# Layer 0's mixture of experts: the second half of two experts' outputs goes back to its nodes by one-hot products instead of a store and gathers

## The chip, the cores and the metric

The kernel runs on one core of a Trainium2 chip. The time is the device time of one execution in microseconds, and the median of several executions is compared. The core has TensorE (PE: matrix products and transposes, into PSUM), VectorE (DVE), ScalarE (ACT), GpSimd (POOL) and SyncE (SP). SP, ACT and POOL issue the transfers (DMA).

## The reference, cut to what matters

Two layers work on 384 nodes with 1024 features each, in float32. Each layer adds a graph block and an attention block to x, and then a mixture of experts. The change lies at the end of layer 0: in its mixture of experts (8 experts, hidden width 352, two experts per node) and in the norm that opens layer 1.

```python
x = x + _L0_ffn_ref(_layernorm(x, axis=-1)[None], ...)[0]     # _L0_ffn_ref:
    top_logits, idx = jax.lax.top_k(logits, TOP_K)            # TOP_K = 2
    scores = jax.nn.softmax(top_logits, axis=-1)
    for e in range(E):                                        # E = 8
        a, g = jnp.split(x_rep @ w1[e].T, 2, axis=-1)
        he = jax.nn.silu(a) * g @ w2[e].T
        out = out + jnp.where((expert_ids == e)[:, None], he, 0)
    out = out * scores.reshape(-1, 1)
    combined = out.reshape(N, TOP_K, h).sum(axis=1)
xn = _layernorm(x, axis=-1)
x = x + _L1_gnn_ref(xn, ...) + _L1_mix_ref(xn[None], ...)[0]
```

So every node's row of x receives two expert rows, each with a weight of its own, before layer 1 can normalize it.

## The kernel before

The nodes lie in three blocks of 128 (NB = 3), one node per partition. x stays in SBUF for the whole run, as does `keep`, a set of small tiles that pass from stage to stage. [...]

**Routing.** `to_places` chooses the two experts of each node and gives it a place in each: expert e has 128 places (CAP0), and place r of expert e is row e * 128 + r of a table in HBM. `keep["slots"]` holds the two row numbers of each node and `keep["share"]` the two weights. The normalized rows are scattered to their places in `xg0`.

**Experts** (`experts0_sorted`). For each expert, `rows_of` loads its 128 rows (POOL's queue) and transposes them on PE (L906). `hidden_of` multiplies them with w1 (L915), and ACT and DVE form the gated hidden rows (L918, L919). `by_feature` transposes these (L925) into `hT` (L926 on DVE, L927 on ACT). The loop runs hidden(e), rows(e + 1), by_feature(e), so that PE has work while the other engines finish. PSUM has three buffers with the tag "t" for all transposes and five with the tag "h" for products. After the loop, for each half and each expert, three products give the expert's 128 x 512 output `y` (L942; the last of the three has depth 96). ACT copies `y` to `ys` (L945) and its own queue stores it in `yg0[hf]` (L946). After the first half, `take(0, nb)` gathers, for each block, the two expert rows of each node from `yg0[0]` (POOL, L306), and DVE adds them to x with their weights (L959).

**The opening of layer 1** (`layer1`). `take(1, nb)` does the same for the second half, just ahead of the norm of the same block: DVE's statistics (L169, L171), ACT's square root (L177), and the norm itself, half on DVE (L201) and half on ACT (L202). `to_t` transposes the normed block on PE (L215, copied by L216), and two halves of products with `w_gnn` follow (L1011). The blocks go one after another; `issue_after` keeps the additions of the next block behind the norm of this one. After the last gather, POOL loads `a_bc` and `ed_w`, and the loads of `w_k` and `w_v` on SP's queue are held until that gather has landed (`held`).

**The order.** Each engine runs its own queue in order. The queues are filled at compile time by a planner, which takes the instructions in the order of the text but lets one go ahead when it expects those before it still to be waiting. Weight tiles come from a ring of buffers, and SP loads the next one as soon as its buffer is free.

Of the kernel before, what the change touches and what calls it, by code (L numbers as in the profile page):

```python
# [10 lines left out]
F32 = mybir.dt.float32  # L11
I32 = mybir.dt.int32
AF = mybir.ActivationFunctionType
OP = mybir.AluOpType
# [3 lines left out]
P = 128  # L18
N = 384
NB = N // P  # L20
D = 1024
KC = D // P
HB = 512
# [5 lines left out]
X = 8  # L29
# [4 lines left out]
CAP0 = 128  # L34
CAP = 64
MORE = 2
LAST = 1
K2 = (128, 128, 96)
PIECE = 1024
# [5 lines left out]
def gps_two_layers(ctx: ExitStack, tc: tile.TileContext, d, out: bass.AP):  # L45
    nc = tc.nc
# [366 lines left out]
    with ExitStack() as layer:  # L413
# [317 lines left out]
        def row(cols, name, dtype=F32):  # L731
            return kp.tile([P, *cols], dtype, name=name)

        keep = {"xe0": [row([KC // 2, P], f"xe0_{g}") for g in range(2)], "oh": row([NB, X], "oh4"), "own": row([NB, P], "own4"), "most": row([NB], "most4"),
                "slot": row([NB], "slot4", I32), "own_e": row([NB], "own_e4", I32), "info": row([NB, 2], "info4"),
                "slots": row([NB, 2], "slots6", I32), "share": row([2, NB], "share6")}


        with tc.tile_pool(name="ps_m0", bufs=4, space=PSUM) as pm, \
# [147 lines left out]
    def experts0_sorted(keep):  # L887

        slots, share = keep["slots"], keep["share"]
        with tc.tile_pool(name="act6", bufs=1) as act, \  # L890
                tc.tile_pool(name="work6", bufs=2) as work, \
                tc.tile_pool(name="ps_t6", bufs=3, space=PSUM) as pt, \
                tc.tile_pool(name="ps_h6", bufs=5, space=PSUM) as ph:

            hT = act.tile([P, X, len(K2), CAP0], F32, name="hT6")

            def rows_of(e):
                if e == 0:
                    return keep["xe0"]
                xs = work.tile([P, D], F32, tag="xs", name="xs6")  # L900
                gp.dma_start(xs, xg0[e * CAP0:(e + 1) * CAP0, :])
                xeT = [work.tile([P, KC // 2, CAP0], F32, tag=f"xeT{g}", name="xeT6") for g in range(2)]
                for g in range(2):
                    ps = pt.tile([P, HB], F32, tag="t", name="t6").rearrange("p (a b) -> p a b", b=P)
                    for j in range(4):
                        nc.tensor.transpose(ps[:, j, :], xs[:, (g * 4 + j) * P:(g * 4 + j + 1) * P], ident)  # L906
                    (ac.copy if g else ve.tensor_copy)(xeT[g], ps)  # L907
                return xeT

            def hidden_of(e, xeT):  # L910
                w1 = [load_w(d["w1s"][e][i], (4, 2 * F0)) for i in range(2)]
                ag = [ph.tile([P, HB], F32, tag="h", name="h6") for _ in range(2)]
                for kc in range(KC):
                    for i in range(2):
                        mm(ag[i][:, :F0], lhsT=xeT[kc // 4][:, kc % 4, :], rhs=w1[kc // 4][:, kc % 4, i * F0:(i + 1) * F0],  # L915
                           start=kc == 0, stop=kc == KC - 1)
                hs = work.tile([P, F0], F32, tag="hs", name="hs6")
                ac.activation(hs, ag[0][:, :F0], AF.Silu)  # L918
                ve.tensor_tensor(hs, hs, ag[1][:, :F0], OP.mult)  # L919
                return hs  # L920

            def by_feature(e, hs):
                ps = pt.tile([P, HB], F32, tag="t", name="t6").rearrange("p (a b) -> p a b", b=P)
                for j, k in enumerate(K2):
                    nc.tensor.transpose(ps[:k, j, :], hs[:, j * P:j * P + k], ident)  # L925
                ve.tensor_copy(hT[:, e, 0:2, :], ps[:, 0:2, :])  # L926
                ac.copy(hT[:K2[2], e, 2, :], ps[:K2[2], 2, :])  # L927

            xeT = rows_of(0)
            for e in range(X - 1):  # L930
                hs = hidden_of(e, xeT)
                xeT = rows_of(e + 1)
                by_feature(e, hs)
            hs = hidden_of(X - 1, xeT)

            for hf in range(2):
                for e in range(X):
                    if e % 2 == 0:
                        w2 = load_w(d["w2s"][hf][e // 2], (2 * len(K2), HB))
                    y = ph.tile([P, HB], F32, tag="h", name="y6")  # L940
                    for j, k in enumerate(K2):
                        mm(y, lhsT=hT[:k, e, j, :], rhs=w2[:k, e % 2 * len(K2) + j, :],  # L942
                           start=j == 0, stop=j == len(K2) - 1)
                    ys = work.tile([P, HB], F32, tag="ys", name="ys6", bufs=5)
                    ac.copy(ys, y)  # L945
                    ac.dma_start(yg0[hf][e * CAP0:(e + 1) * CAP0, :], ys)  # L946
                    if (hf, e) == (0, 0):
                        by_feature(X - 1, hs)
                if hf == 0:
                    for nb in range(NB):  # L950
                        yt = work.tile([P, 2, HB], F32, tag="yt", name="yt6", bufs=3)
                        take(hf, nb, yt)

    def take(hf, nb, yt):

        xs = x[:, nb, hf * HB:(hf + 1) * HB]
        for i in range(2):
            g = gather(yt[:, i, :], yg0[hf][:, :], keep["slots"][:, nb, i:i + 1], X * CAP0)
            ve.scalar_tensor_tensor(xs, yt[:, i, :], keep["share"][:, i, nb:nb + 1], xs, op0=OP.mult, op1=OP.add)  # L959
        return g  # L960


# [19 lines left out]
    def layer1(keep=None):  # L982


        with tc.tile_pool(name="act2", bufs=1) as act, \
# [9 lines left out]

            hn = act.tile([P, NB, KC * K2V], F32, tag="rows3", name="hn")
            ws = [load_w(d["w_gnn"][hf]) for hf in range(2)]
            taken = None
            for nb in range(NB):
                with ExitStack() as behind:  # L1000
                    if nb:
                        behind.enter_context(tc.issue_after(normed_half.ins))
                    if keep is not None:
                        taken = take(1, nb, work.tile([P, 2, HB], F32, tag="xn", name="yt1"))
                    mean, rinv = norm_block(x[:, nb, :])
                    _, normed_half = norm_on_both(xn1[:, nb, :], x[:, nb, :], mean, rinv)
                to_t(pm, xnT, xn1[:, nb, :], nb)
                for hf in range(2):
                    ps = pm.tile([P, HB], F32, tag="mm", name="mm")
                    for kc in range(KC):  # L1010
                        mm(ps, lhsT=xnT[:, kc, nb * P:(nb + 1) * P], rhs=ws[hf][:, kc, :],  # L1011
                           start=kc == 0, stop=kc == KC - 1)
                    ac.copy(hn[:, nb, hf * HB:(hf + 1) * HB], ps)
# [11 lines left out]

            al = row_of(px, "x", alr[:, 0, :])
            for b in range(NB):
                z = part.tile([P, N], F32, tag="z", name="z", bufs=2)
                ve.tensor_scalar(z, al[:, :N], alr[:, 1, b:b + 1], None, op0=OP.add)
                ve.scalar_tensor_tensor(z, z, 0.1, z, op0=OP.mult, op1=OP.max)  # L1030
                ac.activation(z, z, AF.Exp, scale=-1.0)
                ve.tensor_tensor(ed_w[:, b, :], z, ed_w[:, b, :], OP.mult)
# [461 lines left out]
```

## Time and profile before

| what | value |
|---|---|
| time, median of 3 runs | 1063.53 us (1063.5 to 1066.45) |
| profiled execution: its time | 1067.88 us |
| profiled execution: span | 1066.2 us |
| granted TensorE clock, mean | 0.978 |
| last expert product of layer 0 (L942) ends | 698.84 us |
| last store of `yg0[1]` (L946) issued | 699.49 us |
| first gather of the second half (L306) starts | 702.54 us |
| first transpose of layer 1 (L215) starts | 710.69 us |

Times within the span count from its start. A group's row gives source line, engine, operation, the tiles written and read, and the count. A row of the timeline gives start and duration in microseconds, and in square brackets how long the engine had been idle and what ended that. A row of the waits gives the total, the number and the longest. A row of the windows gives the length, then for PE, PEld (weight loads), DVE, ACT and POOL the busy time with the number of instructions, then the granted TensorE clock as a share of full speed, the DMA engines' busy share and GB/s. One product of 128 x 512 in float32 shows as two matmul records.

### The profile page before, as it was taken

To read this page: it belongs to the slowest core of one execution; us is meant where nothing else is said; L and a number is where in the kernel's file an instruction comes from. 1 tells how busy PE (TensorE), PEld (TensorE's weight loads), DVE (VectorE), ACT (ScalarE), POOL (GpSimd) and SP (SyncE) were. 2 spreads that over 40 slices of the span, in tenths; PEclk is the share of its full clock that TensorE was granted. 3 is DMA by queue.
4 is the path that set the end of the run, shared out by engine and by line. 5 is a ranking of instruction groups with operands and counts; after the bars stand their busy time and mean duration, and the time that the engine had idled before them with its cause. 6 is when DMAs were issued, how large, how long until landed. Compare 5 with 4: busy or idle time off the path is not lost. (4 is left out here: it accounts for less than half of the span.)

```text
span 1066.2 us, 9480 instructions
## 1 busy us (share of the span) xinstructions
PE 1017.0 (95%) x3437; PEld 554.8 (52%) x3437; DVE 350.4 (33%) x973; ACT 269.7 (25%) x499; POOL 321.9 (30%) x277
## 2 busy tenths in 40 slices
PE   6999999999999999999998999959999999998895
PEld 4555555544555555544465665424444465555252
DVE  4580000006667766701342110061306000474221
ACT  3111111110876666611131111221302010122120
POOL 2142466566686778500001000130002000013121
PEclk9999999999999999999998999969999999998998
DMA  9939523334425242532365888968522222425994
GB/s 348 401 127 372 146 80 103 135 113 93 77 1 138 22 78 1 159 110 98 113 216 210 300 314 289 393 233 293 197 79 79 79 79 79 158 79 197 388 383 120
DMA packets 69813, 183.35 MB, mean 172 GB/s; under 512 B 21520, under 2 KB 22384, under 8 KB 69504
## 3 DMA queue, kind: packets, MB, share of 16 engines
q1 hardware_dynamic: 40640, 146.01, 38.2%
q0 software_dynamic: 25120, 28.88, 11.6%
q10 hardware_dynamic: 4000, 7.79, 1.9%
q8 instruction: 29, 0.48, 0.2%
q14 instruction: 24, 0.20, 0.1%
HBM read 160.22 MB, written 22.96 MB: 172 GB/s over the span
## 5 line engine op out<-in xcount | busy, mean ns | idle before, releaser
L479 POOL DMA_INDIRECT countd<-seen,cells x96 | 153.2, 1596 | 63.2 <-DMA countd<-seen,cells 38.0
L134 PE MATMUL mm<-xnT,w 128*128 128x384 f32 x512 | 165.7, 486 | 0.0
L665 PE MATMUL mm<-xnT,w 128*128 128x384 f32 x384 | 132.4, 493 | 0.0
L134 PEld LDWEIGHTS mm<-xnT,w 128*128 128x128 f32 x512 | 97.1, 190 | 67.5 <-DVE xnT L216 0.2
L479 POOL DMA_INDIRECT lastd<-typ,cells x96 | 95.1, 991 | 110.0 <-DMA lastd<-typ,cells 70.3
L665 PEld LDWEIGHTS mm<-xnT,w 128*128 128x128 f32 x384 | 70.5, 190 | 56.4 <-issue 13.4
L713 PE MATMUL mm<-w,t 128*128 128x512 f32 x192 | 84.3, 595 | 0.8 <-DVE x L401 0.8
L146 PE MATMUL mm<-w,xnT 128*128 128x512 f32 x192 | 82.8, 592 | 0.0
L134 PE MATMUL mm<-t,w 128*128 128x384 f32 x256 | 82.7, 486 | 0.0
L915 PE MATMUL h<-w,xeT 128*128 128x352 f32 x224 | 68.3, 462 | 0.7 <-DVE xeT L907 0.3
L134 PEld LDWEIGHTS mm<-t,w 128*128 128x128 f32 x256 | 48.6, 190 | 33.9
L146 PEld LDWEIGHTS mm<-w,xnT 128*128 128x128 f32 x192 | 36.3, 190 | 45.5 <-issue 45.5
L713 PEld LDWEIGHTS mm<-w,t 128*128 128x128 f32 x192 | 35.9, 190 | 44.1 <-issue 42.2
L585 DVE TENSOR_TENSOR kind<-last 128x1152 f32<-128x1152 f32 x1 | 1.4, 1359 | 165.3 <-DMA last<-lastd 165.3
L915 PEld LDWEIGHTS h<-w,xeT 128*128 128x128 f32 x224 | 41.9, 190 | 24.4 <-DVE xeT L907 2.4
L291 POOL DMA_INDIRECT xg<-xn,slot x3 | 4.0, 1341 | 140.6 <-DVE xn L1127 135.5
L1011 PE MATMUL mm<-w,xnT 128*128 128x512 f32 x96 | 44.8, 627 | 1.3 <-DVE xnT L216 1.3
L1116 PE MATMUL mm<-w,oT 128*128 128x512 f32 x96 | 42.6, 595 | 0.0
L942 PE MATMUL y<-w,hT 128*128 128x512 f32 (+1 forms) x96 | 41.6, 592 | 0.0
L146 PE MATMUL mm<-w,t 128*128 128x512 f32 x96 | 41.4, 592 | 0.0
L526 ACT ACTIVATE t<-mm,cols 128x384 f32<-128x384 f32 x24 | 13.9, 580 | 106.5 <-PE mm L134 106.5
L1066 POOL TENSOR_TENSOR x<-x,gb 128x1024 f32<-128x1024 f32 x3 | 7.3, 2425 | 101.2 <-DVE x L1065 101.2
(298 smaller groups left out, 1201.6 us busy)
## 6 DMA issues: line engine op xcount, KB each, us to landing
w<-in_w1s SPq DMA_DIRECT2D x16, 1408.0 KB
w<-in_xw SPq DMA_DIRECT2D x8, 2048.0 KB
w<-in_xw2s SPq DMA_DIRECT2D x8, 2048.0 KB
w<-in_w2s SPq DMA_DIRECT2D x8, 1536.0 KB
keys<-keyd POOLq DMA_DIRECT2D x4, 1536.0 KB
xg<-blank SPq DMA_DIRECT2D x12, 512.0 KB
xs<-xg POOLq DMA_DIRECT2D x10, 512.0 KB
w<-in_wk SPq DMA_DIRECT2D x2, 2048.0 KB
```

The source lines that it names most:

```text
L134: mm(ps[:, :N], lhsT=w[:, j, kc, :], rhs=rhs[:, kc, :], start=kc == 0, stop=kc == KC - 1)
L146: mm(ps, lhsT=lhs[:, kc, nb * P:(nb + 1) * P], rhs=w[:, kc, :], start=i == 0 and kc == 0, stop=i == len(pairs) - 1 and kc == KC - 1)
L291: i = gp.indirect_dma_start(rows, bass.IndirectOffsetOnAxis(ap=at, axis=0), src, None, bounds_check=n - 1, oob_is_err=False, compute_op=op)
L479: gp.indirect_dma_start(cells[:, :], bass.IndirectOffsetOnAxis(ap=at[:, i, c:c + 1], axis=0), src[:, c:c + 1], None, bounds_check=N * N + ...
L526: ac.activation(dst[:, ob, :], ps, AF.Identity, bias=cols[:, i, ob:ob + 1], scale=1.0)
L665: mm(ps[:, :N], lhsT=w[:, j, kc, :], rhs=xnT[:, kc, :], start=kc == 0, stop=kc == KC - 1)
L713: mm(pss[hf], lhsT=src[:, kc, nb * P:(nb + 1) * P], rhs=w_out[("mwo", "wo")[part]][hf][:, kc, :], start=part == 0 and kc == 0, stop=part = ...
L915: mm(ag[i][:, :F0], lhsT=xeT[kc // 4][:, kc % 4, :], rhs=w1[kc // 4][:, kc % 4, i * F0:(i + 1) * F0], start=kc == 0, stop=kc == KC - 1)
L942: mm(y, lhsT=hT[:k, e, j, :], rhs=w2[:k, e % 2 * len(K2) + j, :], start=j == 0, stop=j == len(K2) - 1)
L1011: mm(ps, lhsT=xnT[:, kc, nb * P:(nb + 1) * P], rhs=ws[hf][:, kc, :], start=kc == 0, stop=kc == KC - 1)
L1066: gp.tensor_tensor(x[:, b, :], x[:, b, :], gb[:, 1, :], OP.add)
L1116: mm(ps, lhsT=oT[:, kc, nb * P:(nb + 1) * P], rhs=ws[hf][:, kc, :], start=kc == 0, stop=kc == KC - 1)
```

## The change

For the last two experts (BACK = 2: experts 6 and 7) and the second half alone, the output does not go through HBM. ACT copies `y` into the two tiles `keep["xe0"]`, whose former content, the rows of expert 0, is no longer used. A new function `ways_back`, called after `by_feature` of expert 5, builds for each block of nodes a 128 x 256 matrix that has a node's weight at its place in expert 6 or 7 and zeros elsewhere. Six transposes on PE turn these round, and ACT copies them to `keep["back"]`. At the opening of layer 1, two products for each block, `back` with `xe0`, give in PSUM the weighted sum of what experts 6 and 7 return to each node, and DVE adds it to x after the two gathers. The gathers still fetch two rows for each node, out of the first 768 rows: an index that lies in experts 6 and 7 is replaced by row 767 with weight 0 (`slots_g`, `share_g`). `take` receives index, weight and row count as arguments; those of the first half are as before. In the graph block of layer 1, `z` shares its two buffers with `em`.

```diff
+BACK = 2
...
-                "slots": row([NB, 2], "slots6", I32), "share": row([2, NB], "share6")}
+                "slots": row([NB, 2], "slots6", I32), "share": row([2, NB], "share6"), "back": row([BACK, N], "back6"),
+                "slots_g": row([NB, 2], "slots_g6", I32), "share_g": row([2, NB], "share_g6")}
...
+            def ways_back():
+
+                lim = (X - BACK) * CAP0
+                sf = act.tile([P, NB, 2], F32, name="sf6")
+                ve.tensor_copy(sf, slots)
+                low = act.tile([P, NB, 2], F32, name="low6")
+                ve.tensor_scalar(low, sf, float(lim - 1), None, op0=OP.min)
+                ve.tensor_copy(keep["slots_g"], low)
+                ve.tensor_tensor(low, low, sf, OP.is_equal)
+                ve.tensor_tensor(keep["share_g"].rearrange("p i n -> p n i"), low, share.rearrange("p i n -> p n i"), OP.mult)
+                ve.tensor_scalar(sf, sf, float(-lim), None, op0=OP.add)
+                ps = [pt.tile([P, HB], F32, tag="t", name="t6") for _ in range(BACK)]
+                for nb in range(NB):
+                    to = [work.tile([P, BACK * CAP0], F32, tag=f"to{i}", name="to6") for i in range(2)]
+                    for i in range(2):
+                        ve.tensor_scalar(to[i], rowf[:, :BACK * CAP0], sf[:, nb, i:i + 1], share[:, i, nb:nb + 1],
+                                         op0=OP.is_equal, op1=OP.mult)
+                    ve.tensor_tensor(to[0], to[0], to[1], OP.add)
+                    for e in range(BACK):
+                        nc.tensor.transpose(ps[e][:, nb * P:(nb + 1) * P], to[0][:, e * CAP0:(e + 1) * CAP0], ident)
+                for e in range(BACK):
+                    ac.copy(keep["back"][:, e, :], ps[e][:, :N])
...
                 by_feature(e, hs)
+                if e == X - 3:
+                    ways_back()
...
+                    if hf and e >= X - BACK:
+                        ac.copy(keep["xe0"][e - X + BACK].rearrange("p a b -> p (a b)"), y)
+                        continue
                     ys = work.tile([P, HB], F32, tag="ys", name="ys6", bufs=5)
...
-    def take(hf, nb, yt):
+    def take(hf, nb, yt, slots, share, rows):
...
-            g = gather(yt[:, i, :], yg0[hf][:, :], keep["slots"][:, nb, i:i + 1], X * CAP0)
-            ve.scalar_tensor_tensor(xs, yt[:, i, :], keep["share"][:, i, nb:nb + 1], xs, op0=OP.mult, op1=OP.add)
+            g = gather(yt[:, i, :], yg0[hf][:rows, :], slots[:, nb, i:i + 1], rows)
+            ve.scalar_tensor_tensor(xs, yt[:, i, :], share[:, i, nb:nb + 1], xs, op0=OP.mult, op1=OP.add)
...
-            taken = None
+            taken, backs = None, []
+            for nb in range(NB if keep is not None else 0):
+                backs.append(px.tile([P, HB], F32, tag="x", name="back"))
+                for e in range(BACK):
+                    mm(backs[nb], lhsT=keep["back"][:, e, nb * P:(nb + 1) * P],
+                       rhs=keep["xe0"][e].rearrange("p a b -> p (a b)"), start=e == 0, stop=e == BACK - 1)
             for nb in range(NB):
...
-                        taken = take(1, nb, work.tile([P, 2, HB], F32, tag="xn", name="yt1"))
+                        taken = take(1, nb, work.tile([P, 2, HB], F32, tag="xn", name="yt1"),
+                                     keep["slots_g"], keep["share_g"], (X - BACK) * CAP0)
+                        xs = x[:, nb, HB:]
+                        ve.tensor_tensor(xs, xs, backs[nb], OP.add)
...
-                z = part.tile([P, N], F32, tag="z", name="z", bufs=2)
+                z = part.tile([P, HB], F32, tag="em", name="z", bufs=2)[:, :N]
```

More of the change, by code (lines that the diff above doesn't have):

```diff
@@ L951, in experts0_sorted @@
                         yt = work.tile([P, 2, HB], F32, tag="yt", name="yt6", bufs=3)
-                        take(hf, nb, yt)
-    def take(hf, nb, yt):
+                        take(hf, nb, yt, slots, share, X * CAP0)
+    def take(hf, nb, yt, slots, share, rows):
         xs = x[:, nb, hf * HB:(hf + 1) * HB]
         for i in range(2):
-            g = gather(yt[:, i, :], yg0[hf][:, :], keep["slots"][:, nb, i:i + 1], X * CAP0)
-            ve.scalar_tensor_tensor(xs, yt[:, i, :], keep["share"][:, i, nb:nb + 1], xs, op0=OP.mult, op1=OP.add)
+            g = gather(yt[:, i, :], yg0[hf][:rows, :], slots[:, nb, i:i + 1], rows)
+            ve.scalar_tensor_tensor(xs, yt[:, i, :], share[:, i, nb:nb + 1], xs, op0=OP.mult, op1=OP.add)
         return g
```

## The prediction, made before the changed kernel was run

> **What bounds the kernel now.** I read the page first: its engine row says which engine to follow, and its list of waits says where that engine stands still.
>
> ```profile
> span 1066.2 us, 9480 instructions
> PE 1017.0 (95%) x3437; PEld 554.8 (52%) x3437; DVE 350.4 (33%) x973; ACT 269.7 (25%) x499; POOL 321.9 (30%) x277
> ```
>
> TensorE is busy for 95% of the span, so a change pays only by shortening its work, its waits or its slow spells. The waits of PE, longest first:
>
> ```profile
> PE mm L215 <- ACT xn L202: 12.0, 2, 11.9
> ```
>
> One wait of 11.9 us is the largest of all, and it lies where the change works, between the two layers. PE's timeline around it:
>
> ```profile
> 659.98 38.86 PE L942 MATMUL y<-w,hT 128*128 128x512 f32 x90
> 710.69 1.94 PE L215 MATMUL mm<-ident,xn 128*128 128x128 f32 x8 [11.86 <-ACT xn L202]
> 713.16 16.86 PE L1011 MATMUL mm<-w,xnT 128*128 128x512 f32 x32 [0.53 <-DVE xnT L216]
> 729.85 1.04 PE L215 MATMUL mm<-ident,xn 128*128 128x128 f32 x8
> 731.33 13.97 PE L1011 MATMUL mm<-w,xnT 128*128 128x512 f32 x32 [0.44 <-DVE xnT L216]
> ```
>
> The expert products end at 698.84; the first transposes of layer 1 start at 710.69. Also, the first block's work after the gap takes longer than the second's: 1.94 against 1.04 us, and 16.86 against 13.97. The timeline of all engines shows what fills the gap:
>
> ```profile
> 694.33 0.33 ACTq L946 DMA_DIRECT2D yg<-ys  x1
> ...
> 699.49 0.33 ACTq L946 DMA_DIRECT2D yg<-ys  x1
> ...
> 702.54 1.00 POOL L306 DMA_INDIRECT yt<-yg,slots  x1 [8.54 <-DMA yg<-ys]
> ...
> 705.97 0.75 DVE L959 SCALAR_TENSOR_TENSOR x<-yt,share,x 128x512 f32<-128x512 f32 x1 [7.21 <-DMA yt<-yg,slots]
> ...
> 707.35 0.75 DVE L959 SCALAR_TENSOR_TENSOR x<-yt,share,x 128x512 f32<-128x512 f32 x1 [0.63 <-DMA yt<-yg,slots]
> ```
>
> The last expert's store is issued at 699.49, the first gather at 702.54, its two results are used at 705.97 and 707.35, and 3.34 us of norm follow until 710.69. Experts 6 and 7 each cost 2.58 us of PE, so expert 5's store was issued already at 694.33.
>
> The third cost is the clock. The windows view, with PEclk third from the end:
>
> ```profile
> 978.35:981.76 3.41, 0.85 (x6) 0.47 (x7) 1.53 (x2) 2.47 (x8) 2.80 (x4) 1.00 0.53 108
> 981.76:985.18 3.42, 3.42 (x10) 0.98 (x8) 0.00 (x0) 0.00 (x0) 1.31 (x3) 0.50 0.92 296
> 988.59:992.01 3.42, 1.57 (x8) 0.29 (x4) 0.00 (x0) 0.00 (x0) 2.51 (x4) 1.00 0.92 353
> 992.01:995.42 3.41, 1.42 (x8) 0.80 (x9) 1.04 (x5) 0.91 (x4) 0.95 (x1) 1.00 0.96 333
> 995.42:998.83 3.41, 3.41 (x13) 1.65 (x11) 1.67 (x3) 0.79 (x3) 0.00 (x0) 0.50 1.00 386
> 698.46:701.87 3.41, 0.38 (x1) 0.00 (x0) 0.30 (x1) 1.87 (x2) 0.00 (x0) 1.00 0.22 80
> 712.11:715.52 3.41, 2.88 (x6) 1.30 (x5) 2.98 (x8) 1.64 (x3) 0.00 (x0) 0.50 1.02 379
> 715.52:718.94 3.42, 3.42 (x5) 1.35 (x4) 2.89 (x8) 0.35 (x3) 1.08 (x1) 0.50 1.01 400
> ```
>
> The granted clock changes only on a grid of 3.41 us. It halves after a window with PE busy for 0.38, 0.85 or 1.42 us, not after 1.57. It returns after a full window, not after one of 2.88. So the gap cost more than itself: PE ran at half clock from 710.69 to 718.94, which is 0.9 us on the transposes, 2.9 on the products and 0.1 on the wait: 3.9 us.
>
> **The change part by part.**
>
> Removed: of the second half, the stores of experts 6 and 7 (0.33 us each on ACT's queue, 256 KB). They were what the gathers waited for last. The six gathers stay, so POOL and DVE keep all 12 instructions there (about 1.0 and 0.75 us each); only their indices and weights change.
>
> Building the one-hots, ahead of expert 6's hidden products. DVE: six small operations of about 0.2 us (L390 to L397 rows), six 128x256 comparisons of about 0.41 (L387 takes 0.336 at 128x128, L201 0.56 at 128x512), three additions of about 0.41 (between L1102's 0.28 at 128x128 and L228's 0.52 at 128x384): 4.9 us. DVE waits 9.4 us per expert for PE there (65 us over seven experts at L919), so this costs nothing unless PE waits for it. If that cover fails, it is the slow rival below. ACT: two copies of 128x384, at most 0.58 each (L945's wider row), under its 58 us of waits at L918. PE: six transposes in its own queue. Eight at L906 take 0.87 us (635.06 to 635.93), so six take 0.65. I take **+0.8**, between 0.65 and 1.3 if each breaks the stream.
>
> Experts 6 and 7, second half: the ACT copies go to another tile at the same 0.58. SP's queue and the weights are untouched.
>
> The products that give the rows back: six of 128x512. Three such products take 2.58 us at L942, so six take 5.2 us of PE. They need the last ACT copy: from about 700.35 (698.84 + 0.8 + 0.6 for the copy + 0.1) to 705.55. That is inside the old gap, cost 0; without the gap it would be 5.2. Three additions from PSUM are new on DVE, 0.69 each (L401). Only the first stands on the path: **+0.7**. Behind it in DVE's queue is that block's own norm; the other two blocks have 14 us of products as cover.
>
> The start of the gathers. Expert 5's store takes its place as the last. Its time from issue to gather is not shown: the last store, with DMA nearly empty, took 3.05; the last of the first half, issued at 678.85 for a gather at 686.39, took 7.54 at full DMA load. DMA share is 0.88 from 694 to 696, 0.57 from 696 to 698 and 0.22 after, and ACT's packets in one-microsecond windows (144 a store) put expert 5's last data near 697.5: of 343 between 694 and 700 the last 144 are expert 6's, and of the other 199 all but 29 have moved by 697; 1.3 us later (as after the last store's data) is 698.8. With the +0.8 partly absorbed by the emptier queue, I take a gather at **699.2**, 4.1 after its issue, against 702.54: -3.35. The ends are 698.2 and 702.7. The first half's own gathers and additions end at 694.0 on POOL and 698.76 on DVE, ahead of it.
>
> First transposes: 710.69 - 3.35 + 0.7 = 708.0, a gain of **2.7 us**. The +0.8 is inside this number. PE then waits from 705.55 to 708.0: 2.45 us.
>
> The clock. [...] But the row 978.35:981.76 holds a wait of only 2.56 us (L1326) and the clock halved. From the rows, a window with over about 1.9 us idle loses it. [...] If it halves, it does so between 707.45 and 709.5; the next window still holds the 0.5 us wait before L1011, so full clock is back two windows later, near 715.3. Lost: (715.3 - 708.0 - 0.5) / 2 = 3.4, against 3.9 now: gain 0.5. I take the row, not the rule: sum -2.7 - 0.5 = **-3.2 us**.
>
> The shared buffer of z and em has no new waiter: z's last use (L1032, ending at 771.1) is 36 us before em's first (L1061, 807.4). Weight loads held for the last gather (713.13) go out 3 us earlier; their products start after 760, with no PE wait there, so that gives nothing. From layer 1 on PE is almost continuous, so the gain is carried through.
>
> The profiled execution took 1067.88 us (span 1066.2 and 1.7 around it), and becomes 1064.7. The median shown is 1063.53; runs reach 1066.45. I apply the same difference to the median: **1060.3**.
>
> **The rivals.**
>
> Full clock kept (same mechanism, luckier grid, or more PE work in the gap): -2.7 - 3.9 = -6.6, 1056.9. [...] Against: the 2.56 us row.
>
> The store lands late: expert 5's bytes queue behind the gathers of the first half, 7.54 us as at 686.39. The gather is at 702.7 and the transposes at 711.5, +0.8, with the clock between -0.5 and -2: 1062 to 1063.2. Against: DMA's falling share after 696. The change would do on chip what it says, and still not start the gathers earlier.
>
> Slower: PE waits for DVE. If the six transposes are queued right behind expert 5's and DVE starts on the one-hots only then, PE stands for up to the 4.9 us of DVE, plus 0.4 of the copy ahead of it: 5.3. That also halves the clock (about 3.5, as after the big gap). Without shift the gap shrinks by 3.5, so -3.5 + 0.65 - 0.5 + 5.3 + 3.5 = +5.5: 1069.0. It decides from about 2 us of wait in one place, where the clock goes too. For it: PE runs its queue in order. Against: the queue is filled by readiness, not by the text (two products of L915 stand ahead of the L925 transposes at 581.12), and the inputs exist from 564.6.
>
> **How the numbers follow.** Clock halved again 0.45 (1058.8 to 1062), clock kept 0.31 (1055.5 to 1058), store late 0.09, PE behind DVE 0.15. Measurement can tell about 0.3%, 3.2 us: faster means below 1060.3. That takes the whole second case and half of the first: 0.54. The other half and the late store give 0.31 the same, the last case 0.15 slower. The range 1055.8 to 1064.8 leaves out the slow rival and little else.
>
> **What would show it.** Right: the wait at L215 falls from 11.9 to about 2.5 us, with 12 matmul records of 128x512 ahead of it; the first second-half gather starts about 4 us after the last store; six transposes before expert 6 with no PE wait over 0.5 us. PEclk right after the gap tells the first two cases apart. Wrong: a PE wait on the one-hot tiles, a gather still 7 us behind its store, or PE waiting for its products' PSUM.

## The result: the relative gain came as forecast, from a base that was read too low

| kernel | median | runs | lowest to highest |
|---|---|---|---|
| before | 1066.78 us | 22 | 1062.57 to 1069.54 |
| after | 1063.13 us | 22 | 1060.56 to 1065.83 |

The two kernels took turns on one chip. The ratio is 0.9971 (0.996 to 0.9982), which on 1066.8 is -3.1 us (-4.3 to -1.9): just short of the 0.3% that a measurement can tell. (It is not the quotient of the two medians in the table, which are 3.65 us apart.) The forecast was a difference of -3.2 us, and a time of 1060.3. The difference came, and the time was 2.8 us too low. The profiled execution of the changed kernel took 1065.01 us. Its page, first the span and then busy time, share and instructions of each engine:

```profile
span 1063.2 us, 9534 instructions
PE 1023.2 (96%) x3455; PEld 557.6 (52%) x3455; DVE 356.4 (34%) x991; ACT 271.0 (25%) x501; POOL 325.2 (31%) x277
```

TensorE has 6.2 us more busy time and a span that is 3.0 us shorter: the new products are there, and they lie in what was a wait. The page's list of PE's waits (total, number, longest) shows what is left of the 11.9 us:

```profile
PE mm L216 <- DVE xn L202: 3.1, 2, 2.6
...
PE back L1032 <- ACT xe L972: 0.7, 1, 0.7
```

PE's timeline of the changed kernel, from the hidden products of expert 6 to the opening of layer 1:

```profile
637.20 0.44 PE L950 MATMUL t<-ident,to 128*128 128x128 f32 x2
637.48 0.76 PE L917 MATMUL h<-w,xeT 128*128 128x352 f32 x2
638.07 0.38 PE L950 MATMUL t<-ident,to 128*128 128x128 f32 x2
...
661.31 38.86 PE L969 MATMUL y<-w,hT 128*128 128x512 f32 x90
700.85 5.42 PE L1032 MATMUL back<-xe,back 128*128 128x512 f32 x12 [0.68 <-ACT xe L972]
708.86 1.09 PE L216 MATMUL mm<-ident,xn 128*128 128x128 f32 x8 [2.60 <-DVE xn L202]
710.72 16.98 PE L1049 MATMUL mm<-w,xnT 128*128 128x512 f32 x32 [0.76 <-DVE xnT L217]
727.54 1.04 PE L216 MATMUL mm<-ident,xn 128*128 128x128 f32 x8
```

The transposes of the one-hots (L950) stand two at a time between products of expert 6, with no idle time ahead of them. From the end of the last expert product (700.17) to the first transposes of layer 1 (708.86) it is 8.69 us instead of 11.85; in that time the products of the way back take 5.42 and PE waits 0.68 and 2.60. The timeline of the other engines in that stretch:

```profile
695.67 0.33 ACTq L976 DMA_DIRECT2D yg<-ys  x1
...
697.63 1.54 DVE L989 SCALAR_TENSOR_TENSOR x<-yt,share,x 128x512 f32<-128x512 f32 x2 [0.25 <-DMA yt<-yg,slots]
700.07 1.00 POOL L307 DMA_INDIRECT yt<-yg,slots_g  x1 [4.78 <-DVE x L989]
...
703.77 0.75 DVE L989 SCALAR_TENSOR_TENSOR x<-yt,share_g,x 128x512 f32<-128x512 f32 x1 [4.60 <-DMA yt<-yg,slots_g]
...
705.03 0.75 DVE L989 SCALAR_TENSOR_TENSOR x<-yt,share_g,x 128x512 f32<-128x512 f32 x1 [0.52 <-DMA yt<-yg,slots_g]
705.92 0.69 DVE L1042 TENSOR_TENSOR x<-x,back 128x512 f32<-128x512 f32 x1
```

The store of expert 5 is now the last of the second half (columns 512 to 1023 of a row, `hf` 1), and the first gather follows 4.40 us after its issue. The chain is the same as before (store, gather, two additions, norm), with one addition more, and it starts earlier. The windows on the grid of the clock (in this profile all eleven changes of the granted clock, from 559.74 to 1058.09, lie on one grid of 3.41 us; PE's busy time second, PEclk third from the end):

```profile
703.10:706.52 3.42, 3.17 (x8) 1.14 (x6) 2.10 (x3) 0.00 (x0) 2.45 (x3) 1.00 0.60 164
706.52:709.93 3.41, 1.07 (x8) 0.85 (x8) 2.94 (x8) 1.11 (x2) 2.92 (x4) 1.00 0.62 191
709.93:713.34 3.41, 2.65 (x4) 1.17 (x4) 2.98 (x6) 0.88 (x2) 0.00 (x0) 0.50 1.04 380
713.34:716.76 3.42, 3.42 (x5) 1.35 (x4) 3.31 (x7) 0.82 (x2) 0.70 (x1) 0.50 0.99 387
716.76:720.17 3.41, 3.41 (x9) 1.52 (x8) 1.85 (x6) 0.30 (x1) 0.62 (x1) 1.00 1.04 410
```

One window with PE busy for only 1.07 us, and the clock is halved for the next two, one of which held 2.65 us of work. So this execution fell in the likelier of the forecast's two cases. The window that lost the clock held 2.34 us of the first wait (706.52 to 708.86) and nothing of the second.

### The profile page after: what moved, and what is told of

The parts are those of the page before. It is cut to its first block, busy times and chain, and to the rows that moved or that the text cites. A ratio compares the mean times of both kernels' runs of the same rounds, so it can differ in the third digit from the quotient of the medians.

```text
span 1063.2 us, 9534 instructions
## 1 busy us (share of the span) xinstructions
PE 1023.2 (96%) x3455; PEld 557.6 (52%) x3455; DVE 356.4 (34%) x991; ACT 271.0 (25%) x501; POOL 325.2 (31%) x277
```

## The experiments

The theory to test: the gain is the earlier start of the gathers, because the last store in front of them is expert 5's; what PE does for the way back lies in the old gap; and most executions still pay for a halved clock. The rivals: the gain is only another placing of the clock's grid; the new products and transposes cost what the earlier start brings; something else in the stretch (a buffer, the order of the queues) sets the start.

Three measures are used. The ratio is to the kernel before on the same chip. The **stretch** is read from the one profile: from the first expert output product (`y`) to the transposes of the second node block, which holds the whole gap and the slow spell behind it. The **lost clock** is (1 - granted clock) x span, the mean over all runs of a kernel. Idle time at half clock counts in it too, so it tells how often the clock falls, not what it costs. The intervals come from all runs, the stretch and every row below from a single execution.

| kernel | ratio (95%) | runs | stretch, us | lost clock, us |
|---|---|---|---|---|
| before | 1 | 51, 50, 36, 14 | 72.78 | 23.2, 23.5, 22.6, 24.3 |
| after | 0.9971 (0.996 to 0.9982) | 22 | 69.14 | 17.9 |
| after_again | 0.9968 (0.9954 to 0.9982) | 22 | 69.02 | 17.6 |
| late_stores | 1.0012 (1.0 to 1.0024) | 14 | 73.09 | 18.7 |
| no_return | 0.996 (0.9945 to 0.9975) | 14 | 69.89 | 20.9 |
| back1 | 0.998 (0.997 to 0.9989) | 22 | 70.06 | 20.2 |
| warm_before | 0.9988 (0.9977 to 0.9999) | 22 | 69.07 | 17.0 |
| warm_after | 0.9952 (0.9933 to 0.997) | 6 | 70.17 | 15.0 |
| free_buffer | 0.9962 (0.9949 to 0.9975) | 10 | 69.38 | 18.3 |
| free_warm | 0.9968 (0.9956 to 0.998) | 17 | 69.63 | 16.6 |
| kept_clock | 0.9959 (0.9942 to 0.9975) | 18 | 67.01 | 15.2 |
| fill_turns | 0.9951 (0.9933 to 0.9969) | 11 | 67.77 | 14.7 |
| kept_before | 0.9981 (0.9959 to 1.0003) | 14 | 69.19 | 15.5 |
| turns_free | 0.9969 (0.994 to 0.9997) | 9 | 67.15 | 15.7 |

**The changed kernel once more (after_again).** No edit.

> The changed kernel once more, as the mark for the other runs of this series. Theory A (the gathers start 2.5 us earlier, and the clock still halves in the gap in most executions): about 3 us under the kernel before, -0.3%; the first transposes 8.7 us after the last expert product, and the first block's products (L1049) at 17.0 or at 14.0 us according to whether the clock halved. Theory B (the time came from elsewhere, for instance from fewer bytes in the transfers): the same total, but then the runs below don't follow the gap and the clock.

Measured: 1063.44 us, -0.32%, and a stretch of 69.02 against 69.14. The result repeats.

**The two stores put back, everything else kept (late_stores).**

```diff
-                    if hf and e >= X - BACK:
-                        ac.copy(keep["xe0"][e - X + BACK].rearrange("p a b -> p (a b)"), y)
-                        continue
                     ys = work.tile([P, HB], F32, tag="ys", name="ys6", bufs=5)
...
                     ac.dma_start(yg0[hf][e * CAP0:(e + 1) * CAP0, :], ys)
+                    if hf and e >= X - BACK:
+                        ac.copy(keep["xe0"][e - X + BACK].rearrange("p a b -> p (a b)"), y)
+                        continue
...
-                                     keep["slots_g"], keep["share_g"], (X - BACK) * CAP0)
+                                     keep["slots_g"], keep["share_g"], X * CAP0)
```

> The changed kernel, but the second half of experts 6 and 7 is stored to HBM as before as well (in addition to the copies that stay on chip), and the gathers wait for these stores too. The products and additions of the change stay. Theory A: the early start of the gathers is the gain, so it is gone: the first transposes come 11.9 us after the last expert product, plus 0.7 for the addition, 12.5 in all; the clock halves as in the kernel before; with the six transposes (0.6) the total is 1.3 us above the kernel before (+0.1%) and over 4 us above the changed kernel. A rival, C (the six products in the gap help by themselves, since PE idles less): 1 to 3 us faster than the kernel before, without the early gathers.

Measured: 1067.25 us, +0.12%. The timeline of late_stores, POOL and PE:

```profile
702.00 5.42 PE L1032 MATMUL back<-xe,back 128*128 128x512 f32 x12 [1.16 <-ACT xe L975]
...
704.71 0.99 POOL L307 DMA_INDIRECT yt<-yg,slots_g  x1 [8.64 <-issue]
...
713.50 1.97 PE L216 MATMUL mm<-ident,xn 128*128 128x128 f32 x8 [6.09 <-DVE xn L202]
```

The products of the way back are at the same place behind the expert products and take the same 5.42 us, and yet the transposes come 12.66 us after the last expert product (700.84) instead of 8.69. With the wait for two stores put back the whole gain is gone. So the earlier start is the gain, and with the old start what the change adds costs 0 to 0.24%. The clock is not what makes the difference: at 18.7 us, late_stores loses little more of it than the changed kernel does.

**The way back left out (no_return).** The calls that form and use it are removed:

```diff
-                ve.tensor_scalar(sf, sf, float(-lim), None, op0=OP.add)
-                ps = [pt.tile([P, HB], F32, tag="t", name="t6") for _ in range(BACK)]
...
-                    ac.copy(keep["back"][:, e, :], ps[e][:, :N])
...
-            for nb in range(NB if keep is not None else 0):
-                backs.append(px.tile([P, HB], F32, tag="x", name="back"))
...
-                        xs = x[:, nb, HB:]
-                        ve.tensor_tensor(xs, xs, backs[nb], OP.add)
```

> The changed kernel without the one-hot matrices, their six transposes, the six products and the three additions: what experts 6 and 7 give in the second half is left out of the result. The stores are gone and the gathers start early as in free_buffer, but PE has nothing to do in the gap. Theory A: transposes 7.5 us after the last expert product, 1.2 earlier than in the changed kernel, and 0.6 saved upstream, but with a pure gap of 7.5 us the clock halves in every execution (3.4 us against 60% of 3.4): 0.5 us under the changed kernel, -0.36%. Rival (the one-hot return has a price that the gap does not hide): 2 us or more under the changed kernel, -0.5% or better.

Measured: -0.40%. The timeline of no_return, POOL and PE:

```profile
699.87 1.00 POOL L307 DMA_INDIRECT yt<-yg,slots_g  x1 [5.49 <-DVE x L977]
...
708.26 1.94 PE L216 MATMUL mm<-ident,xn 128*128 128x128 f32 x8 [8.95 <-DVE xn L202]
710.74 16.87 PE L1030 MATMUL mm<-w,xnT 128*128 128x512 f32 x32 [0.53 <-DVE xnT L217]
```

PE waits 8.95 us in one piece and its transposes then take 1.94 us, against 1.09 in the changed kernel's profile at full clock. Against the changed kernel's -0.29% this is some 1.1 us, with intervals that overlap. That is about the 0.6 of the six transposes and the 0.7 of the addition, but the profile does not show it so: the transposes were expected 7.5 us after the last expert product and came after 8.94, no earlier than the 8.69 of the changed kernel. The gather started 5.06 us after expert 5's store was issued (694.81), against 4.40, because the store's last packet came 3.8 us after its issue, against 2.7. No cost of the 5.4 us of products can be seen; what the 1.1 us are made of stays open.

**One expert instead of two (back1).**

```diff
-BACK = 2
+BACK = 1
```

> The changed kernel with BACK = 1: only expert 7's second half stays on chip. Theory A: the gathers wait for expert 6's store, issued 2.58 us later but landing in 3.1 instead of 4.4, so the gather starts 1.4 later than in the changed kernel; three products (2.6 us) stand in the gap, PE waits about 6.5 us in one piece and the clock always halves: 2.4 us over the changed kernel, -0.07% against the kernel before. Rival (the gain goes with the bytes that are not stored): half of the changed kernel's gain, -0.16%.

Measured: -0.20% (-0.30 to -0.11), better than expected. The timeline of back1, PE and POOL:

```profile
699.34 2.84 PE L1032 MATMUL back<-xe,back 128*128 128x512 f32 x6 [0.68 <-ACT xe L972]
699.64 0.99 POOL L307 DMA_INDIRECT yt<-yg,slots_g  x1 [5.93 <-DMA yg<-ys]
708.70 1.97 PE L216 MATMUL mm<-ident,xn 128*128 128x128 f32 x8 [6.52 <-DVE xn L202]
```

With half of the products the wait is 6.52 us and the transposes take 1.97 us, as at half clock (1.94 in the kernel before). By the time alone, the rival (half of the gain for half of the bytes, -0.16%) fits better than the theory, whose -0.07% lies outside the interval. The profile speaks for the theory's chain: the gather started 2.91 us after the store of expert 6 (696.73), the one now last, and the transposes came 10.04 us after the last expert product, 1.35 us later than in the changed kernel, where 1.4 was expected. The part that was wrong is the clock: it was counted as if the changed kernel mostly kept it, but that loses it nearly as often (80% of its executions by the estimate under kept_clock). An edit that cuts the bytes and leaves the start alone was not tried.

**The old gap filled with products in the kernel before (warm_before).** Eleven products whose result is not used stand ahead of the loop over the blocks:

```diff
+            if keep is not None:
+                spare_ps = px.tile([P, HB], F32, tag="x", name="fill")
+                for i in range(11):
+                    mm(spare_ps, lhsT=ident, rhs=ws[0][:, i % KC, :], start=True, stop=True)
```

> The kernel before, with 11 products of 128 x 512 on data that is at hand put into the gap behind the last expert product; their result is not used. Nothing else is changed: stores, gathers and additions stay. Theory A says that half of what the gap costs is the clock: the 11 products (9.5 us) end near the old start of the transposes, PEclk stays 1.00, the first block's products fall from 16.9 to 14.0 us and its transposes from 1.9 to 1.0, and the whole is 3.5 us faster than the kernel before (-0.33%), with less spread. Theory B (the first block is slow because of the transfers that run beside it, w_k and w_v at full DMA load, not because of the clock): no gain, or up to 0.5 us slower where the products run past the old start.

Measured: -0.12% (-0.23 to -0.01), less than expected. PE's timeline of warm_before:

```profile
699.38 9.71 PE L1002 MATMUL fill<-w,ident 128*128 128x512 f32 x22 [0.68 <-ACT ys L945]
710.32 1.09 PE L215 MATMUL mm<-ident,xn 128*128 128x128 f32 x8 [1.23 <-DVE xn L201]
712.17 14.00 PE L1015 MATMUL mm<-w,xnT 128*128 128x512 f32 x32 [0.76 <-DVE xnT L216]
```

In this execution the clock was kept: 1.09 us for the transposes and 14.00 for the products, and a stretch 3.7 us shorter. The lost clock of 17.0 us says that it was not kept in all: the kernels with both waits filled, below, lose about 15.0. What is left idle here is 1.23 + 0.76 = 1.99 us within one window's length, close to the forecast's edge of about 1.9. Why 3.7 us of the stretch gave only some 1.3 us in the runs stays open.

**Two unused products behind the six of the way back (warm_after)**, in the changed kernel.

```diff
+            if keep is not None:
+                spare_ps = px.tile([P, HB], F32, tag="x", name="fill")
+                for i in range(2):
+                    mm(spare_ps, lhsT=ident, rhs=ws[0][:, i, :], start=True, stop=True)
```

> The changed kernel with 2 unused products of 128 x 512 behind the six that bring the rows back; they fill 1.7 of the 2.6 us for which PE waits. Theory A: no window of 3.41 us with more than 1.9 us idle remains, so PEclk stays 1.00 in every execution and the first block takes 14.0 us; where the changed kernel loses the clock (estimated 60% of executions, 3.4 us each) this is gained: 2 us on the mean under the changed kernel, 5 us under the kernel before (-0.5%). Theory B: the same as the changed kernel.

Measured: -0.48%, but from six runs, and a stretch that is longer than that of the changed kernel, not shorter. The timeline of warm_after, DVE and PE:

```profile
711.41 0.73 DVE L989 SCALAR_TENSOR_TENSOR x<-yt,share_g,x 128x512 f32<-128x512 f32 x1
712.07 0.68 DVE L217 COPY xnT<-mm 128x512 f32<-128x512 f32 x1
712.80 15.70 PE L1053 MATMUL mm<-w,xnT 128*128 128x512 f32 x32 [1.42 <-DVE xnT L217]
```

The planner put an addition of the next block ahead of the copy that PE waits for. The second wait grew from 0.76 to 1.42 us, and the 32 records take 15.70 us instead of the 14.00 of warm_before: the clock was halved for a part of them in spite of the filling. In this execution the first gather also came 6.00 us after expert 5's store (695.42 to 701.42) instead of 4.40, a delay larger than the 1.0 us by which the stretch grew. An edit on PE changed DVE's order, so this run does not test the filling alone.

**A scratch buffer taken away (free_buffer).** In the changed kernel the gather started 1.65 us after the last packet on the queue of the store it waits for (698.4), in the kernel before 1.3. One of the one-hot tiles gets one buffer instead of two:

```diff
-                    to = [work.tile([P, BACK * CAP0], F32, tag=f"to{i}", name="to6") for i in range(2)]
+                    to = [work.tile([P, BACK * CAP0], F32, tag=f"to{i}", name="to6", bufs=2 - i) for i in range(2)]
```

> The changed kernel with one buffer instead of two for the second of the one-hot scratch tiles (1 KB less in that stage). In the changed kernel the first gather of the second half starts 0.90 us after DVE's last addition of the first half in the profiles (0.97 and 0.90 in two more), and the planner's list of its waits names DVE and all gather lanes: its target lies where the stage before kept its last gather buffer. With 1 KB less the two don't overlap and the list keeps the stores. Theory D (that buffer wait holds the gather): the gather starts 0.5 to 1 us earlier against the last expert product, PE's wait falls from 2.6 to about 1.9 us and the clock is kept more often: 1.3 us under the changed kernel, -0.45% against the kernel before. Rival (the store of expert 5 lands last anyway): the same as the changed kernel, -0.32%.

Measured: -0.38%. Timeline of free_buffer, the first gather:

```profile
696.85 0.99 POOL L307 DMA_INDIRECT yt<-yg,slots_g  x1 [5.21 <-DVE x L989]
```

The last packet was at 695.6, so it is 1.25 us now. It is so in every kernel: 1.15 to 1.35 us with less of this scratch or none (the kernel before, warm_before, kept_before, no_return, back1, free_buffer, free_warm, turns_free), 1.55 to 1.65 with all of it (after, after_again, late_stores, warm_after, kept_clock, fill_turns). That is about 0.4 us on the chain that a scratch tile of another stage costs. The row above names DVE's last addition of the first half, but a wait for it does not explain the difference: in late_stores that addition had ended 4.4 us before the gather (700.30), and the distance is 1.55 all the same. How the tile does it no trace shows. In the time it can't be told apart: -0.38 against -0.29 and -0.32%.

**Both together (free_warm).** free_buffer with warm_after's two products.

> The same as free_buffer, with the two unused products of warm_after behind the six. Theory A and D together: the gather at its free start, and no window with 1.9 us idle, so the clock stays in every execution: transposes about 8.2 us after the last expert product, first block's products 14.0 us; 6 us under the kernel before (-0.57%). If the buffer wait does not matter: as warm_after, -0.48%.

Measured: -0.32%, well short of it. PE's timeline of free_warm, and two of its windows:

```profile
709.28 1.09 PE L216 MATMUL mm<-ident,xn 128*128 128x128 f32 x8 [2.02 <-DVE xn L202]
...
708.96:712.38 3.42, 1.68 (x10) 1.20 (x11) 3.38 (x7) 1.04 (x2) 1.18 (x2) 1.00 0.83 283
712.38:715.79 3.41, 3.41 (x6) 1.35 (x5) 2.98 (x8) 1.12 (x2) 0.00 (x0) 0.50 0.98 342
```

A wait of 2.02 us ahead of the transposes and one of 1.42 behind them remained, and the clock was halved from 712.38 to 715.79. The window ahead of that held 0.32 us of the first wait (708.96 to 709.28) and the whole second: neither wait lay in it with more than 1.42 us, and together they lost the clock. Filling a part of one wait was not enough here, with the other in the same window of 3.42 us. With 1.74 us idle, this window also lies under the forecast's edge, an estimate of about 1.9 from the rows with 1.42 and 1.57 us busy.

**Both waits filled and DVE's order held (kept_clock).** Three unused products behind the six, one behind the transposes of the first block, and the next block's additions held behind the first copy:

```diff
+                for i in range(3):
+                    mm(spare_ps, lhsT=ident, rhs=ws[0][:, i % KC, :], start=True, stop=True)
...
-                        behind.enter_context(tc.issue_after(normed_half.ins))
+                        behind.enter_context(tc.issue_after(copied[0].ins))
...
+                copied, turned = to_t(pm, xnT, xn1[:, nb, :], nb)
+                if keep is not None and nb == 0:
+                    with tc.issue_after(turned.ins):
+                        for i in range(1):
+                            mm(spare_ps, lhsT=ident, rhs=ws[0][:, i, :], start=True, stop=True)
```

> The changed kernel with three unused products behind the six (2.6 us, all of PE's wait) and one more between the first block's transposes and its products (0.8 us wait there); DVE's additions for the next block are held behind the first block's copy from PSUM, which the products had otherwise pushed back. Clock lost per run is summed as (1 - granted clock) times the span: 17.7 us for the changed kernel, about 14.5 of it outside the gap (23.3 of the kernel before, less 8.5 in its gap). Theory A2 (transposes don't keep the clock, so the wait, the transposes and the next wait, 4.5 us, lose it in nearly every execution of the changed kernel; with all but the 1.1 us of transposes filled it is kept): lost clock falls to 14.5 us, the first block takes 14.0 us in the profile, and the whole is 2 to 3 us under the changed kernel, -0.5% to -0.6% against the kernel before. Rival (the earlier unused products gained little because they cost something themselves): no better than -0.35%.

Measured: -0.41%. PE's timeline of kept_clock:

```profile
705.20 2.74 PE L1037 MATMUL fill<-w,ident 128*128 128x512 f32 x6
708.98 1.09 PE L216 MATMUL mm<-ident,xn 128*128 128x128 f32 x8 [1.04 <-DVE xn L202]
709.91 1.02 PE L1053 MATMUL fill<-w,ident 128*128 128x512 f32 x2
710.77 13.90 PE L1057 MATMUL mm<-w,xnT 128*128 128x512 f32 x32
```

The 32 records take 13.90 us, about what the second block's took in the kernel before (13.97), and the lost clock falls to 15.2 us (14.7 in the next run). So, if these two never lose it here, about 15 us of lost clock belong to the rest of the kernel, and the changed kernel's 17.6 to 17.9 hold 2.6 to 2.9 us from this place. One fall takes two windows at half clock in the profile of the changed kernel, 3.41 us lost. That gives an estimate of 80% of the executions; with the spread of the runs it can be anything from 50% to all.

**The same with transposes instead of products (fill_turns).**

```diff
-                for i in range(3):
-                    mm(spare_ps, lhsT=ident, rhs=ws[0][:, i % KC, :], start=True, stop=True)
+                for i in range(22):
+                    nc.tensor.transpose(spare_ps[:, i % 4 * P:(i % 4 + 1) * P], ws[0][:, i % KC, :P], ident)
```

> The same as kept_clock, but PE's wait is filled with 22 unused transposes (2.4 us) in place of the three products; PE is as busy as there. Theory A2 (transposes don't count for the clock): the clock is lost as in the changed kernel, lost clock 17.5 us or more, time as the changed kernel, -0.3%. Rival (what counts is that PE is busy): as kept_clock, 14.5 us.

Measured: -0.49%, lost clock 14.7 us. PE's timeline of fill_turns, and two of its windows:

```profile
703.63 2.57 PE L1037 MATMUL fill<-ident,w 128*128 128x128 f32 x22
708.19 1.09 PE L216 MATMUL mm<-ident,xn 128*128 128x128 f32 x8 [1.99 <-DVE xn L202]
709.12 1.02 PE L1053 MATMUL fill<-w,ident 128*128 128x512 f32 x2
709.98 13.90 PE L1057 MATMUL mm<-w,xnT 128*128 128x512 f32 x32
...
704.21:707.62 3.41, 1.99 (x19) 1.75 (x17) 2.66 (x7) 0.29 (x1) 2.41 (x3) 1.00 0.55 165
707.62:711.03 3.41, 2.84 (x13) 1.87 (x14) 2.66 (x6) 1.40 (x2) 1.47 (x3) 1.00 0.89 333
```

The first of the two windows holds transposes alone, 1.99 us of them, and the next one still runs at full clock. So in this execution the transposes kept the clock as the three products did in kept_clock, and the theory that transposes don't count did not come true: the fall in the changed kernel is not to be put down to their kind. The single wait of 1.99 us (706.20 to 708.19) kept the clock here, but an edge of the windows at 707.62 cuts it into 1.42 and 0.57. That in some executions of the changed kernel the second wait of 0.76 us adds to the first is likely from free_warm, but not shown; no run filled that one alone.

**The kernel before with both waits filled (kept_before).** Twelve products in the gap, one behind the transposes, DVE's order held.

> The kernel before with the gap filled like that: 12 unused products behind the last expert product, one behind the first block's transposes, and the same hold on DVE. In warm_before 1.2 us of wait, the transposes and 0.8 us of wait were left open, and lost clock was 17.0 where 14.5 was expected. Theory A2: lost clock 14.5 us, 3 us under the kernel before (-0.3%), without any of the change. Rival (the clock in the gap is worth less in timed executions than in the profiled one): -0.12% as warm_before.

Measured: -0.19% (-0.41 to +0.03). The lost clock is 15.5 us and the stretch 3.6 us shorter, near the 3.9 that the forecast put on the slow spell. In the time it stays open: the interval holds both the expected -0.3% and nothing. So a shorter stretch does not show in the runs with its full size, here or in warm_before.

**fill_turns with free_buffer (turns_free).**

> The two improvements together: fill_turns (PE's wait filled with 22 unused transposes and one product, DVE held behind the first copy) with the smaller scratch of free_buffer. In the kernels with the long list of waits the gather starts 1.7 to 1.8 us after the store's last packet, in those without it 1.2 to 1.3. So: gather within 1.3 us of the last packet, clock kept, lost clock about 15 us (17.7 in the changed kernel), and 5 to 6 us under the kernel before: -0.5% to -0.55%. If the buffer wait is worth nothing in time: as fill_turns, -0.49%; if the filling is not worth its place either, the changed kernel's -0.3%.

Measured: -0.31% (-0.60 to -0.03) from nine runs. The gather follows the last packet by 1.2 us and the lost clock is 15.7 us, but no gain over fill_turns can be seen. None of the filled kernels is shown to be faster than the changed kernel: all their intervals overlap its own. By the stretch, kept_clock is 2.0 to 2.1 us shorter.

## Why the prediction was wrong, and what in it was right

**The base, the step that failed.** The text said: "I apply the same difference to the median", and took 1063.53, a median of three runs. In 22 runs the kernel before has a median of 1066.78, so this term of the sum was 3.25 us too small; the later batches gave 1066.6 to 1067.4. The 22 runs lie in bunches: six from 1062.57 to 1064.07, eleven from 1065.97 to 1067.43, five from 1069.16 to 1069.54. Two of the first three belong to the lowest bunch. (In the batch of 51 that stands beside after_again, the 13 runs below 1064.2 lost 21.8 us of clock and the 26 around 1067.5 lost 23.9; what else parts the bunches stays open.) The profiled execution pointed higher (1067.88), and the text had worked out its own result, 1064.7, and set it aside; the profiled execution of the changed kernel took 1065.01. From the true median the same difference gives 1063.6, against 1063.13 measured: the base is more than the whole miss of 2.8 us.

The wrong base carried into the cases. Below 1060.3 the forecast called the result faster, with the highest chance, 0.54; that did not come. The likeliest mechanism, the clock halved again, stood at 1058.8 to 1062, and 1063.13 lies outside it, in the numbers of the late store (1062 to 1063.2). By its time alone the result would have been put down to the wrong cause; the gather 4.40 us after its store, where the late store would have taken 7.54, tells them apart.

**The start of the gathers, right.** Forecast: gather 4.1 us after expert 5's store, transposes at 708.0. Measured: 4.40 us, and 708.86, of which 0.71 is a later start of the whole stage in that execution (expert 6's rows are transposed at 635.77 instead of 635.06): 708.15. The 0.3 us more between store and gather is no more than what the scratch tile costs (0.4, free_buffer). The 4.1 was no sure thing: it was 4.3 to 4.4 in the profiles of after, after_again and free_buffer, and 5.1 to 6.1 in those of no_return, free_warm, turns_free, kept_clock, warm_after and fill_turns. late_stores showed that this start is all of the gain.

**Six transposes, a little too much.** Forecast +0.8 (0.65 to 1.3). Expert 6's hidden products with the transposes among them take 10.19 us (637.20 to 647.39), without them 9.57 (636.49 to 646.06): 0.62, just under the range. PE's queue did not wait for DVE: five of the six comparisons, 0.41 us each as forecast, ran from 572.8 on, so the slow rival had no place to happen.

**Products and addition, right.** 5.42 us against 5.2, in the gap; 0.69 against 0.7. The wait of PE is 2.60 against 2.45.

**The clock, the right case, from an estimate that is too sharp.** Forecast: a fall in about 60% (0.45 against 0.31 for the clock kept), and then 6.8 us at half clock, from about 708.5 to 715.3. Measured: 709.93 to 716.76 in the profile, falls in the profiles of after_again and free_buffer too, and an estimate of 80% that leaves 60% possible. No run shows the 60% itself: it took the grid of the clock to lie anywhere with the same chance. What the profiles show is an edge at 709.93 us of the span in the changed kernel, at 708.96 in free_warm, at 707.62 in fill_turns and at 712.11 in the kernel before: four places, and no two of them are whole windows of 3.41 us apart. The working took the 2.45 us alone and let the wait behind the transposes only delay the return; in free_warm a window with 0.32 us of one wait and 1.42 of another lost it. The sum barely moves, since it was made for the case with the fall. The edge of "about 1.9 us idle" is no sharp one: a window of the changed kernel with PE busy for 1.45 us (986.41:989.82) kept the clock, its next with 1.51 (989.82:993.23) lost it, and so did one with 1.68 (free_warm). And the rows shown were not all of the falls. The profile before has this one as well:

```profile
968.11:971.52 3.41, 3.04 (x28) 2.80 (x26) 2.47 (x6) 0.88 (x2) 2.94 (x2) 1.00 1.02 417
971.52:974.94 3.42, 2.65 (x13) 2.55 (x13) 2.56 (x22) 2.64 (x5) 0.00 (x0) 0.50 0.11 43
```

PE counts as busy for 3.04 us of the first window, the last 1.8 of them with products only 8 columns wide (L1150), and the clock halves. In the changed kernel it halves after a window with PE busy for all 3.41 us (556.33:559.74), the last 2.5 of them with products 8 columns wide (L787, L385, L342). So idle time is not all that counted here; what else did was not tested. Nor did the clock come back after full windows alone: in the profile before it was back at 1.00 behind one with PE busy for 3.00 us (974.94:978.35).

The rival with the full clock kept (-6.6) did not come in the profile: behind a wait of 2.60 us stands a window at 0.50.

**Carried through, right.** From the expert outputs on, the changed profile is 3.64 us ahead at the second block's transposes (72.78 - 69.14). Less the 0.62 upstream, that is 3.0 (2.5 from the earlier start and 0.5 from the clock, where 2.7 and 0.5 were forecast), and the span is 3.0 us shorter. That the two agree to the tenth is luck: this execution entered the stage 0.71 us late, and the span does not show it.

## What to carry to other kernels

When the wait at a stage's end is for the last store of a chain, take the last items off the chain and bring them back on an engine that stands idle there. Here the gain came from the earlier start of what waits, not from the work saved, and it shrank on the way: against the last expert product, the last store was issued 5.2 us earlier, the gather started 3.8 us earlier and the transposes 3.2. Work out a difference within one profiled execution, but put it on a base of many runs: three runs of a kernel that spreads over 7 us can't carry a forecast of 3. An added scratch tile can delay an instruction of another stage, here the first gather by about 0.4 us.

## What the runs showed of the hardware that was not expected

- In free_warm the clock halved after a window (708.96:712.38) that held 0.32 us of one wait and 1.42 of another. In the profiles of the kernel before and of the changed kernel, past the first 20 us of the span, all eight windows at full clock with PE busy for less than 1.45 us were followed by half clock (the longest 1.42). Windows with 1.45 us (changed, 986.41:989.82) and 1.57 us (before, 988.59:992.01) kept it, one with 1.51 us (changed, 989.82:993.23) and one with 1.68 us (free_warm) lost it. Windows with PE busy for 3.04 us (before, 968.11:971.52) and for all 3.41 us (changed, 556.33:559.74), much of both with products 8 columns wide, lost it too.
- In fill_turns a window with 1.99 us of float32 transposes and nothing else on PE (704.21:707.62) was followed by full clock; over all runs the lost clock was 14.7 us, against 15.2 with products in their place (kept_clock).
- Part of the spread of 5 to 7 us between runs of one kernel went with the clock: over the 22 runs of the changed kernel the span grew by about 0.5 us for each microsecond of lost clock.
- The first gather of the second half, which depends on a store, started 1.15 to 1.35 us after the last packet on the store's queue in the eight kernels with less of the one-hots' scratch or none, and 1.55 to 1.65 us after it in the six with the whole of it, for a reason that no trace shows.
